# Order of work around fc2, the next image's layernorm and k's last tile in a fused transformer and ConvNeXt kernel

## The chip, the cores and the metric

The kernel runs on one core of a Trainium2 chip. The metric is the device time of one execution in microseconds (us). The kernel before ran beside each variant on the same chip; a comparison of two sets of runs goes by their ratios to it.

## The reference, cut to what matters

Eight images of 384 channels and 32 x 32 positions pass through an attention block with an MLP, then through a ConvNeXt block. All is float32.

```python
# layer 0, for each image: N = 1024 tokens, C = 384, 8 heads of 48, hidden 1536
xn  = layernorm(xf, g1, beta1)
q, k, v = split(einsum('bnc,oc->bno', xn, w_qkv) + b_qkv)
out = softmax(q @ k.T * 48 ** -0.5) @ v
x1  = einsum('bnc,oc->bno', out, w_proj) + b_proj + xf
h   = gelu(einsum('bnc,oc->bno', layernorm(x1, g2, beta2), w_fc1) + b_fc1)
y   = x1 + einsum('bnh,oh->bno', h, w_fc2) + b_fc2
# layer 1, on y as an image
z = layernorm(depthwise_conv_7x7(y) + dw_b, ln_w, ln_b)
z = gelu(z @ w1 + b1)
gx = sqrt(sum over positions of z ** 2);  nx = gx / (mean(gx) + 1e-6)
out = y + (grn_gamma * (z * nx) + grn_beta + z) @ w2 + b2
```

## The kernel before

TensorE does all matmuls; the 7 x 7 convolution of one image runs on VectorE (L769) beside the matmuls of the next. In fc2, w1 (called h) and w2, two thirds of the work is done by Strassen's scheme: products of blocks (A11, A12, S1 to S4, A22), for which VectorE must first subtract blocks of the activations (t1 to t4). The last third is done the plain way and is called "straight".

In these traces TensorE and VectorE work through their instructions in the order in which the program emits them: in the kernel before, a variance matmul that waits 3.74 us holds up the ready matmuls behind it. That order is set by a model clock: each group of matmuls calls `flow.pe(us)`, and "chains" (generators: the next image's layernorm, the block differences) emit their next instructions when the clock passes the pause that they yielded. A paced chain counts its pauses from its own last step, an unpaced one from the clock. The pauses therefore move instructions in the queues; they don't delay anything on the chip by themselves. Layernorm sums over channels, which lie on partitions, by a matmul with ones: `total` gives the mean and `var` the variance, so TensorE waits at these two if VectorE is late (28.5 and 33.5 us in the kernel before).

```python
# U = 0.857: model time in us of one full fp32 matmul of 512 columns
class Flow:
    def __init__(self):
        self.now, self.n, self.due, self.inside = 0.0, 0, [], False
    def pe(self, us):
        self.now += us
        if self.inside:
            return
        self.inside = True
        while self.due and self.due[0][0] <= self.now:
            at, _, chain, paced = heapq.heappop(self.due)
            self._step(chain, at, paced)
        self.inside = False
    def _step(self, chain, at, paced):
        wait = next(chain, None)
        if wait is not None:
            self.n += 1
            heapq.heappush(self.due, ((at if paced else self.now) + wait, self.n, chain, paced))
    def spawn(self, chain, paced=False):
        self._step(chain, self.now, paced)
        return chain
    def finish(self, chain):
        if chain is None:
            return
        self.due = [d for d in self.due if d[2] is not chain]
        heapq.heapify(self.due)
        inside, self.inside = self.inside, True
        for _ in chain:
            pass
        self.inside = inside
# ... (cut)
def layernorm(src, dst, h, eps, g, name, switch, spare=False, spaced=False):
    cols = half(h)
    if spare:
        a, *squares = (attn[:, i, :] for i in range(4))
        rstd = a
    else:
        a = one.tile([P, NH], F32, tag="ln_a", name=f"{name}_a{h}")
    nc.vector.tensor_tensor(a, src[:, 0, cols], src[:, 1, cols], ALU.add)
    nc.vector.tensor_tensor(a, a, src[:, 2, cols], ALU.add)
    yield 1.8
    total = o_tile(f"{name}_sum{h}")
    nc.tensor.matmul(out=total, lhsT=ones, rhs=a, start=True, stop=True)
    flow.pe(U)
    yield 0.8
    for ct in range(CT):
        nc.vector.scalar_tensor_tensor(dst[:, ct, cols], total, -1.0 / C, src[:, ct, cols], ALU.mult, ALU.add)
    yield 0.8
    if not spare:
        squares = [three.tile([P, NH], F32, tag="ln_sq", name=f"{name}_sq{h}_{ct}") for ct in range(CT)]
    for ct in range(CT):
        nc.scalar.activation(squares[ct], dst[:, ct, cols], AF.Square)
        if spaced:
            yield 1.7
    yield 0.8 if spaced else 1.8
    nc.vector.tensor_tensor(squares[0], squares[0], squares[1], ALU.add)
    nc.vector.tensor_tensor(squares[0], squares[0], squares[2], ALU.add)
    yield 1.8
    var = o_tile(f"{name}_var{h}")
    nc.tensor.matmul(out=var, lhsT=ones, rhs=squares[0], start=True, stop=True)
    flow.pe(U)
    yield 0.8
    if not spare:
        rstd = one.tile([P, NH], F32, tag="ln_rstd", name=f"{name}_rstd{h}")
    if switch:
        ln_table()
    nc.scalar.activation(rstd, var, AF.Ln, bias=eps, scale=1.0 / C)
    nc.scalar.activation(rstd, rstd, AF.Exp, scale=-0.5)
    yield 2.6 if switch else 1.2
    for ct in range(CT):
        nc.vector.scalar_tensor_tensor(dst[:, ct, cols], dst[:, ct, cols], col(g, ct), rstd, ALU.mult, ALU.mult)
def abreast(*args):
    chains = [layernorm(*args[:2], h, *args[2:], spare=(h == 1)) for h in range(2)]
    while chains:
        waits = []
        for chain in list(chains):
            wait = next(chain, None)
            if wait is None:
                chains.remove(chain)
            else:
                waits.append(wait)
        if waits:
            yield max(waits)
def both(*args):
    for h in range(2):
        yield from layernorm(*args[:2], h, *args[2:])
# ... (cut)
def qk(b, xn):
    big = one.tile([P, HT * N], F32, tag="big", name=f"qk_{b}")
    parts = big[:, : 2 * NP * N].rearrange("p (i m n) -> p i m n", i=2, m=NP)
    for m in range(CT):
        for i in range(2):
            at = i * CT + m
            def evict(dst, ps):
                nc.scalar.activation(dst, ps, AF.Identity, bias=bqk[:, at : at + 1], scale=1.0 if i else SCALE)
            args = lambda k: wqk_sb[:, k, at, :], lambda k: xn[:, k, :], CT
            if (m, i) != (CT - 1, 1):
                evict(parts[:, i, m, :], linear(*args, f"qk_{b}_{at}"))
                continue
            for h in range(2):
                evict(parts[:, i, m, half(h)], linear_half(*args, h, f"qk_{b}_{at}_{h}"))
    for i in range(2):
        for own, other in pieces(lambda m: parts[:, i, m, :]):
            nc.sync.dma_start(out=own, in_=other)
    return parts[:, 0], parts[:, 1]
# ... in attention(): ps_s has two buffers; scores() is one group of 4 matmuls and its exponential
steps = [(qh, m, t) for qh in range(2) for m in ORDER for t in range(KT)]
ln_table()
ln = None
for n in range(len(steps) + 2):
    if n < len(steps):
        ps[n] = scores(*steps[n])
    if n >= 2:
        product(*steps[n - 2], ps.pop(n - 2))
    # ... (cut)
# ... in the MLP: Strassen's form of fc2 for two thirds of the rows, "straight" for the last third
def down(hid, t1, weights, wname, first, add, done, name):
    h = HT // 2
    def block(s, n):
        return [hid[:, s * h + k, half(n)] for k in range(h)]
    def a(key):
        return [weights.at(wname, key)[:, k, :] for k in range(h)]
    def product(key, blocks):
        bank = o_tile(f"{name}_{key}")
        accumulate(bank, list(zip(a(key), blocks)))
        weights.used(wname, key)
        return bank
    straight = ps_s.tile([P, 2, NH], F32, tag="s", name=f"{name}_straight")
    for s, key in enumerate(("A31", "A32")):
        for k in range(h):
            for n in range(2):
                nc.tensor.matmul(
                    out=straight[:, n, :],
                    lhsT=a(key)[k],
                    rhs=block(s, n)[k],
                    start=s + k == 0,
                    stop=s == 1 and k == h - 1,
                )
            flow.pe(2 * U)
        weights.used(wname, key)
    for n in range(2):
        first(2, n, straight[:, n, :])
        done(2, n)
    b11, b12, b21, b22 = (block(s, n) for s in range(2) for n in range(2))
    t3, t2, t4 = b12, b11, b21
    def differences(dst, one_, other):
        for k in range(h):
            nc.vector.tensor_tensor(dst[k], one_[k], other[k], ALU.subtract)
            yield 1.2
    making_t3 = flow.spawn(differences(t3, b22, b12), paced=True)
    p1 = product("A11", b11)
    u2 = two.tile([P, NH], F32, tag="r", name=f"{name}_u2")
    nc.scalar.copy(u2, p1)
    for k in range(h):
        nc.vector.tensor_tensor(t2[k], b22[k], t1[k], ALU.subtract)
    first(0, 0, product("A12", b21))
    add(0, 0, u2)
    done(0, 0)
    making_t4 = flow.spawn(after(making_t3, differences(t4, b21, t2)), paced=True)
    p5 = product("S1", t1)
    first(1, 1, p5)
    first(0, 1, p5)
    add(0, 1, product("S4", b22))
    p6 = product("S2", t2)
    nc.vector.tensor_tensor(u2, p6, u2, ALU.add)
    add(0, 1, u2)
    done(0, 1)
    flow.finish(making_t3)
    p7 = product("S3", t3)
    u3 = two.tile([P, NH], F32, tag="r", name=f"{name}_u3")
    nc.vector.tensor_tensor(u3, p7, u2, ALU.add)
    add(1, 1, u3)
    done(1, 1)
    flow.finish(making_t4)
    first(1, 0, product("A22", t4))
    add(1, 0, u3)
    done(1, 0)
# ... in the loop over the images
def next_norms(b):
    if b > 0:
        acc = state["acc"]
        flow.finish(state["conv"])
        state["norm3"] = flow.spawn(
            sequence(abreast(acc, acc, eps1, "lnw", f"ln3_{b - 1}", True), block_differences(acc))
        )
    if b + 1 < B:
        xn = state["xn"] = load_x(b + 1, "xn")
        state["norm1"] = flow.spawn(
            after(state["norm3"], both(xn, xn, eps0, "g1", f"ln1_{b + 1}", True), 0 if b else 6)
        )
```

## Time and profile before

| | before |
|---|---|
| median of 3 runs, us | 3506.55 (3503.75 to 3507.19) |
| span of the profiled run, us | 3505.6 |
| TensorE busy | 97% |
| VectorE busy | 73% |
| ScalarE busy | 37% |
| ScalarE table loads | 79 |

How to read the lines in this document. A waits line says which engine and instruction (with its line in the kernel, such as L352) waited for which other: us in total, how many times, the longest. A timeline line has the start and the length in us, the engine, the line, the operation, what it wrote and read, its tile and how many records it covers; in brackets stands the idle time of that engine just before, and what ended it. One fp32 matmul is two records: the six of q/k's last tile are the 12 of L309 in the prediction's timeline. The kernel before and the changed one have different line numbers: L335 and L352 (mean and variance) before are L345 and L362 after; scores are L495 and L509; the reads of the straight product are L689 and L705. The lines of the kernel before are shown in the prediction.

### The profile page before, as it was taken

How to read it: one execution, taken by the hardware profiler on the slowest of the kernel's cores; microseconds unless marked ns; L12 is line 12 of the kernel's file. 1: busy time of each engine (PE TensorE's matmuls, PEld its weight loads, DVE VectorE, ACT ScalarE, POOL GpSimd, SP SyncE). 2: the span in 40 equal slices, each digit the busy share in tenths (PEclk: the TensorE clock that was granted, in tenths of full speed). 3: DMA queues.
4: the chain of work that ended last, by engine and by line, in shares of the span. 5: the costliest groups of instructions: out<-in, count | busy, mean ns of one | idle time of the engine just before them, and what ended most of it. 6: DMA issues, size and time to landing. Idle time of an engine off the chain costs nothing.

```text
span 3505.6 us, 36066 instructions
## 1 busy us (share of the span) xinstructions
PE 3397.9 (97%) x14106; PEld 1427.3 (41%) x14106; DVE 2548.4 (73%) x3176; ACT 1293.1 (37%) x1607; POOL 7.7 (0%) x21
## 2 busy tenths in 40 slices
PE   8999999999999999999999999999999999999978
PEld 3334434443344433444334443444434444344433
DVE  3243798677876878768686696857788679959974
ACT  3442353324533154341543405424253332532131
POOL 0000000000000000000000000000000000000000
PEclk9999999999999999999999999999999999999999
DMA  3312101221013200132002320022201312022111
GB/s 114 111 39 76 55 20 49 92 70 36 21 53 96 81 19 17 57 110 66 19 13 67 99 71 14 21 66 92 72 15 32 100 59 58 17 62 81 58 50 42
DMA packets 110688, 200.86 MB, mean 57 GB/s; under 512 B 30768, under 2 KB 37040, under 8 KB 110128
## 3 DMA queue, kind: packets, MB, share of 16 engines
q1 hardware_dynamic: 109936, 196.01, 19.1%
q8 instruction: 113, 1.85, 0.2%
q10 hardware_dynamic: 576, 2.48, 0.2%
q14 instruction: 63, 0.52, 0.1%
HBM read 160.16 MB, written 28.57 MB: 54 GB/s over the span
## 4 chain that ended last, share of the span: by engine, by line
PE 80%; DVE 14%; DMA 2%; ACT 2%; SPq 1%; issue 1%; DVEq 0%; ACTq 0%
PE fc L309 13%; PE h L316 11%; PE o L515 11%; PE s L495 10%; PE qk L296 6%; DVE wqkv L769 5%; PE o_straight L633 4%; PE o_S L316 4%; PE v L424 4%; PE fc_S L316 3%; PE o_A L316 3%; PE fc_straight L633 3%; PE proj L438 3%; DVE acc L769 2%; PE fc_A L316 1%; PE ln_var L352 1%
## 5 line engine op out<-in xcount | busy, mean ns | idle before, releaser
L769 DVE SCALAR_TENSOR_TENSOR acc<-pad,vec,acc 128x1024 f32<-128x1024 f32 x1008 | 1234.7, 1276 | 0.0
L504 ACT ACTIVATE p<-s 128x1024 f32<-128x1024 f32 x512 | 523.3, 1024 | 384.3 <-PE s L495 384.0
L495 PE MATMUL s<-qk 48*64 48x512 f32 x4096 | 532.8, 591 | 10.7 <-ACT p L504 10.7
L515 PE MATMUL o<-p,v 64*64 64x512 f32 x4096 | 530.6, 590 | 0.0
L309 PE MATMUL fc<-xn,fc 128*128 128x512 f32 x1152 | 500.9, 593 | 0.0
L817 DVE TENSOR_TENSOR y<-h,y 128x512 f32<-128x512 f32 x336 | 232.0, 691 | 138.3 <-PE h L316 123.7
L309 PEld LDWEIGHTS fc<-xn,fc 128*128 128x128 f32 x1152 | 218.1, 190 | 277.7 <-issue 274.8
L495 PEld LDWEIGHTS s<-qk 48*64 48x64 f32 x4096 | 153.1, 133 | 300.8 <-issue 271.4
L515 PEld LDWEIGHTS o<-p,v 64*64 64x64 f32 x4096 | 153.7, 132 | 288.0 <-issue 284.2
L600 ACT ACTIVATE hid<-fc,bfc_f 128x512 f32<-128x512 f32 x192 | 131.2, 687 | 361.1 <-PE fc L309 360.3
L296 PE MATMUL qk<-xn,wqkv 128*128 128x512 f32 x480 | 207.4, 592 | 0.0
L316 PE MATMUL h<-acc,w_A 128*128 128x512 f32 x432 | 204.0, 592 | 0.0
L402 ACT ACTIVATE qk<-qk,bqk 128x1024 f32<-128x1024 f32 (+1 forms) x56 | 55.6, 992 | 379.3 <-DVE acc L769 177.3
L769 DVE SCALAR_TENSOR_TENSOR wqkv<-pad,vec,wqkv 128x416 f32<-128x416 f32 (+1 forms) x288 | 191.6, 752 | 0.0
L456 DVE TENSOR_TENSOR attn<-o,attn 128x512 f32<-128x512 f32 x64 | 44.1, 689 | 196.6 <-ACT attn L454 196.6
L633 PE MATMUL o_straight<-y,w_A 128*128 128x512 f32 x336 | 148.5, 602 | 2.2 <-DVE w_A L895 2.2
L633 PE MATMUL fc_straight<-hid,fc_A 128*128 128x512 f32 x336 | 147.5, 592 | 0.0
L296 PEld LDWEIGHTS qk<-xn,wqkv 128*128 128x128 f32 x480 | 91.1, 190 | 114.1 <-issue 113.8
L795 ACT ACTIVATE y<-y,b_f 128x1024 f32<-128x1024 f32 x84 | 96.6, 1150 | 109.8 <-DVE y L817 109.8
L438 PE MATMUL proj<-attn,wproj_sb 128*128 128x512 f32 x288 | 131.4, 609 | 4.3 <-DVE attn L482 3.9
L424 PE MATMUL v<-wqkv,xn 128*128 128x384 f32 x384 | 128.9, 494 | 0.6 <-DVE xn L364 0.6
L316 PEld LDWEIGHTS h<-acc,w_A 128*128 128x128 f32 x432 | 82.1, 190 | 103.3 <-issue 84.7
(205 smaller groups left out, 3311.2 us busy)
## 6 DMA issues: line engine op xcount, KB each, us to landing
w_A<-in_w SPq DMA_DIRECT2D x96, 384.0 KB, 3.2
fc<-in_wfc SPq DMA_DIRECT2D x54, 384.0 KB, 3.4
fc_A<-in_wfc SPq DMA_DIRECT2D x47, 384.0 KB, 3.2
xn<-in_x SPq DMA_DIRECT2D x16, 768.0 KB, 6.7
x<-in_x SPq DMA_DIRECT2D x16, 768.0 KB, 6.6
kept<-x SPq DMA_DIRECT2D x8, 1536.0 KB, 5.8
res<-kept SPq DMA_DIRECT2D x48, 256.0 KB, 3.0
out_y<-res SPq DMA_DIRECT2D x48, 256.0 KB, 2.1
```

What stands on the lines that cost most here:

```text
L296: nc.tensor.matmul(out=ps[:, half(h)], lhsT=lhsT(k), rhs=rhs(k)[:, half(h)], start=(k == 0), stop=(k == nk - 1),)
L309: nc.tensor.matmul(out=ps, lhsT=lhsT(k), rhs=rhs(k)[:, half(h)], start=(k == 0), stop=(k == nk - 1))
L316: nc.tensor.matmul(out=bank, lhsT=lhsT, rhs=rhs, start=k == 0, stop=k == len(pairs) - 1)
L424: nc.tensor.matmul(out=ps[:, :C], lhsT=xn[:, k, t * P : (t + 1) * P], rhs=wv_sb[:, k, :], start=(k == 0), stop=(k == CT - 1),)
L438: nc.tensor.matmul(out=ps, lhsT=wproj_sb[:, m, ct * P : (ct + 1) * P], rhs=attn[:, m, :], start=(m == 0), stop=(m == CT - 1),)
L495: nc.tensor.matmul(out=s[64 * i : 64 * i + 64, j, :], lhsT=kT[64 * j : 64 * j + HD, m, k0 : k0 + 64], rhs=qT[64 * j : 64 * j + HD, m, half ...
L504: nc.scalar.activation(p, s, AF.Exp)
L515: nc.tensor.matmul(out=outs[i][64 * j : 64 * j + 64, :], lhsT=v[keys, t, at : at + 64], rhs=p[keys, j, :], start=(t == 0), stop=(t == KT - 1),
L600: nc.scalar.activation(hid[:, m, half(h)], ps, AF.Gelu, bias=bfc1[:, m : m + 1])
L633: nc.tensor.matmul(out=straight[:, n, :], lhsT=a(key)[k], rhs=block(s, n)[k], start=s + k == 0, stop=s == 1 and k == h - 1,)
L769: nc.vector.scalar_tensor_tensor(dst, window, tap, dst, ALU.mult, ALU.add)
L817: nc.vector.tensor_tensor(dst, bank, part, ALU.add)
```

## The change

The intent: (1) let the differences t2, t3 and t4 of fc2 leave VectorE one after the other in one paced chain, where t2 came as a bulk of six and t3 started beside it; (2) put the next image's layernorm at longer steps (most pauses times 1.8) and the convolution's layernorm too (all pauses times 1.4); the first pause is 2.6 for 1.8 in every layernorm, the second one of each image included; (3) compute k's last tile behind the first two score groups, so that the first exponentials run beside it; (4) leave out a table load of ScalarE where the table of Ln and Exp is still in place.

```diff
     def ln_table():
-        nc.scalar.preload_act_table_set("natural_log_exp_and_others")
-
-    def layernorm(src, dst, h, eps, g, name, switch, spare=False, spaced=False):
+        if table[0] != "ln":
+            nc.scalar.preload_act_table_set("natural_log_exp_and_others")
+        table[0] = "ln"
+
+    def other_table(dst, src, function, **kw):
+        nc.scalar.activation(dst, src, function, **kw)
+        table[0] = None
+
+    def layernorm(src, dst, h, eps, g, name, switch, spare=False, spaced=False, slow=1.0):
 ... (cut)
-        yield 1.8
+        yield 2.6 * slow
         total = o_tile(f"{name}_sum{h}")
 ... (cut)
-        yield 0.8
+        yield 0.8 * slow
 ... (cut)
-        yield 0.8 if spaced else 1.8
+        yield 0.8 if spaced else 1.8 * slow
         nc.vector.tensor_tensor(squares[0], squares[0], squares[1], ALU.add)
         nc.vector.tensor_tensor(squares[0], squares[0], squares[2], ALU.add)
-        yield 1.8
+        yield 1.8 * slow
 ... (cut)
-        yield 2.6 if switch else 1.2
+        yield (2.6 if switch else 1.2) * slow
 ... (cut: in abreast)
-                yield max(waits)
+                yield 1.4 * max(waits)
 ... (cut: in qk)
-                for h in range(2):
-                    evict(parts[:, i, m, half(h)], linear_half(*args, h, f"qk_{b}_{at}_{h}"))
-        for i in range(2):
-            for own, other in pieces(lambda m: parts[:, i, m, :]):
+        moves = [(own, other) for i in range(2) for own, other in pieces(lambda m: parts[:, i, m, :])]
+        for own, other in moves[:-2]:
+            nc.sync.dma_start(out=own, in_=other)
+
+        def last_tile():
+
+            for h in range(2):
+                evict(parts[:, 1, CT - 1, half(h)], linear_half(*args, h, f"qk_{b}_last_{h}"))
+            for own, other in moves[-2:]:
                 nc.sync.dma_start(out=own, in_=other)
 ... (cut: in attention)
         for n in range(len(steps) + 2):
+            if n == 2:
+                last_tile()
             if n < len(steps):
                 ps[n] = scores(*steps[n])
 ... (cut: GELU and square root now go through other_table)
 ... (cut: in down)
-        making_t3 = flow.spawn(differences(t3, b22, b12), paced=True)
         p1 = product("A11", b11)
         u2 = two.tile([P, NH], F32, tag="r", name=f"{name}_u2")
         nc.scalar.copy(u2, p1)
-        for k in range(h):
-            nc.vector.tensor_tensor(t2[k], b22[k], t1[k], ALU.subtract)
+        making_t2 = flow.spawn(differences(t2, b22, t1), paced=True)
+        making_t3 = flow.spawn(after(making_t2, differences(t3, b22, b12)), paced=True)
+        making_t4 = flow.spawn(after(making_t3, differences(t4, b21, t2)), paced=True)
         first(0, 0, product("A12", b21))
         add(0, 0, u2)
         done(0, 0)
-        making_t4 = flow.spawn(after(making_t3, differences(t4, b21, t2)), paced=True)
         p5 = product("S1", t1)
         first(1, 1, p5)
         first(0, 1, p5)
         add(0, 1, product("S4", b22))
+        flow.finish(making_t2)
         p6 = product("S2", t2)
 ... (cut: in next_norms)
-                    after(state["norm3"], both(xn, xn, eps0, "g1", f"ln1_{b + 1}", True), 0 if b else 6)
+                    after(state["norm3"], both(xn, xn, eps0, "g1", f"ln1_{b + 1}", True, slow=1.8), 0 if b else 6)
```

More of the change, by code (lines that the diff above doesn't have):

```diff
@@ L317, in accumulate @@
             flow.pe(U)
+    table = [None]
     def ln_table():
-        nc.scalar.preload_act_table_set("natural_log_exp_and_others")
-    def layernorm(src, dst, h, eps, g, name, switch, spare=False, spaced=False):
+        if table[0] != "ln":
[5 more added lines that the diff above has]
+    def layernorm(src, dst, h, eps, g, name, switch, spare=False, spaced=False, slow=1.0):
         cols = half(h)
@@ L377, in abreast, with both @@
             if waits:
-                yield max(waits)
-    def both(*args):
+                yield 1.4 * max(waits)
+    def both(*args, slow=1.0):
         for h in range(2):
-            yield from layernorm(*args[:2], h, *args[2:])
+            yield from layernorm(*args[:2], h, *args[2:], slow=slow)
     def pieces(at):
@@ L406, in qk @@
                     evict(parts[:, i, m, :], linear(*args, f"qk_{b}_{at}"))
-                    continue
-                for h in range(2):
-                    evict(parts[:, i, m, half(h)], linear_half(*args, h, f"qk_{b}_{at}_{h}"))
-        for i in range(2):
-            for own, other in pieces(lambda m: parts[:, i, m, :]):
+        moves = [(own, other) for i in range(2) for own, other in pieces(lambda m: parts[:, i, m, :])]
[5 more added lines that the diff above has]
+            for own, other in moves[-2:]:
                 nc.sync.dma_start(out=own, in_=other)
-        return parts[:, 0], parts[:, 1]
+        return parts[:, 0], parts[:, 1], last_tile
     def heads(t):
@@ L482, in average, with attention @@
         nc.vector.tensor_tensor(attn[:, m, :], attn[:, m, :], r, ALU.mult)
-    def attention(b, xt, qT, kT, xn, first=None):
+    def attention(b, xt, qT, kT, last_tile, xn, first=None):
         sums = two.tile([P, 2 * NP * 8], F32, tag="sums", name=f"sums_{b}")
@@ L599, in gelu_half @@
         ps = linear_half(lambda k: w[:, k, :], lambda k: xn[:, k, :], CT, h, f"{name}_{h}_{m}")
-        nc.scalar.activation(hid[:, m, half(h)], ps, AF.Gelu, bias=bfc1[:, m : m + 1])
+        other_table(hid[:, m, half(h)], ps, AF.Gelu, bias=bfc1[:, m : m + 1])
     def spare_blocks(name):
@@ L794, in finish @@
         def finish(m):
-            nc.scalar.activation(y[:, m, :], y[:, m, :], AF.Gelu, bias=b1[:, m : m + 1])
+            other_table(y[:, m, :], y[:, m, :], AF.Gelu, bias=b1[:, m : m + 1])
         def squares(i):
@@ L849, in grn_up_straight @@
                 ps = linear(lambda k: raw[:, tiles[k], :], lambda k: acc[:, k, :], CT, f"h_{b}_{m}")
-                nc.scalar.activation(y[:, m, :], ps, AF.Gelu, bias=b1[:, m : m + 1])
+                other_table(y[:, m, :], ps, AF.Gelu, bias=b1[:, m : m + 1])
                 nc.scalar.activation(ps, y[:, m, :], AF.Square, accum_out=gx[:, m : m + 1])
@@ L873, in grn_scale @@
         wb = f"w2_{tag}"
-        nc.scalar.activation(gx, gx, AF.Sqrt)
+        other_table(gx, gx, AF.Sqrt)
         yield 6.5
@@ L1145, in main @@
         for b in range(B):
-            qT, kT = qk(b, state["xn"])
+            qT, kT, last_tile = qk(b, state["xn"])
             if b == 0:
@@ L1150, in main @@
             xn = one.tile([P, CT, N], F32, tag="xn", name=f"xn2_{b}")
-            ln2, rest = attention(b, xt, qT, kT, xn, folding if b == 0 else None)
+            ln2, rest = attention(b, xt, qT, kT, last_tile, xn, folding if b == 0 else None)
             if b < B - 1:
@@ L1194, in exact_path @@
         with tc.For_i(0, B) as b:
+            table[0] = None
             weights = Weights(plan_fc1("x") + plan_fc2_fast("x") + plan_w1("x") + plan_w2("x"))
@@ L1198, in exact_path @@
             values("x", xn)
-            exact_attention(xt, *qk("x", xn))
+            qT, kT, last_tile = qk("x", xn)
+            last_tile()
+            exact_attention(xt, qT, kT)
             xn = one.tile([P, CT, N], F32, tag="xn", name="xn2_x")
```

## The prediction

> **What bounds the kernel now.** I read the page's busy shares and the slices of the span first, then the list of waits for TensorE alone, then the timeline around each wait.
>
> ```profile
> span 3505.6 us, 36066 instructions
> PE 3397.9 (97%) x14106; PEld 1427.3 (41%) x14106; DVE 2548.4 (73%) x3176; ACT 1293.1 (37%) x1607; POOL 7.7 (0%) x21
> ...
> PEclk9999999999999999999999999999999999999999
> ```
>
> TensorE is busy 97% of the span at a full granted clock. It is the bound, and all that a reordering can win lies in its 3505.6 - 3397.9 = 107.7 us of idle time. The reader should see from this alone that 2% (70 us) is out of reach unless two thirds of the idle time goes.
>
> The waits of TensorE (who, for whom: us in total, times, longest):
>
> ```profile
> PE ln_var L352 <- DVE ln_sq L349: 33.5, 11, 3.7
> PE ln_sum L335 <- DVE ln_a L332: 28.5, 11, 15.0
> PE s L495 <- ACT p L504: 10.7, 9, 1.2
> ```
>
> I placed every TensorE gap in the timeline. The start takes 15.3 us (load, first layernorm) and everything after the last image's fc2 42.5 us (the last convolution, the last scaling, the end); the change touches neither. The other 49.8 us are small gaps, of which these matter:
> - 1.24 us before the third score tile, once in each of 8 images: 9.9 us.
> - In fc2 of images 1 to 6, 3.74 us before the next layernorm's first variance sum (22.4 us) and, in four of them, 0.71, 0.85, 0.85 and 0.37 us before its second mean (2.8 us): 25.2 us. In image 0, 0.55 + 2.68 = 3.2 us.
> - In the second layernorm: 0.38, 0.62 and 1.50 us in image 1, 0.39 in image 6, 0.65 and 0.81 in image 7.
>
> The timeline of image 2's fc2 shows the 3.74:
>
> ```profile
> 1048.32 2.74 PE L316 MATMUL fc_A<-hid,fc_A 128*128 128x512 f32 x6
> ...
> 1050.89 1.40 DVE L689 SCALAR_TENSOR_TENSOR x<-fc_straight,vec,x 128x512 f32<-128x512 f32 x2
> 1051.03 1.13 PE L335 MATMUL ln_sum<-ln_a,ones 128*128 128x512 f32 x2
> ...
> 1057.01 3.69 DVE L659 TENSOR_TENSOR hid<-hid,fc_t 128x512 f32<-128x512 f32 x6
> ...
> 1062.01 0.69 DVE L349 TENSOR_TENSOR ln_sq<-ln_sq,ln_sq 128x512 f32<-128x512 f32 x1
> 1062.76 2.08 PE L352 MATMUL ln_var<-ln_sq,ones 128*128 128x512 f32 x2 [3.74 <-DVE ln_sq L349]
> ```
>
> VectorE has six block differences in a bulk (L659) and more of L651 ahead of the sum of squares, and TensorE meets the variance matmul before they are done.
>
> The timeline at the scores of image 3:
>
> ```profile
> 1249.48 1.11 ACT L402 ACTIVATE qk<-qk,bqk 128x1024 f32<-128x1024 f32 x1 [4.03 <-PE qk L296]
> ...
> 1254.63 0.69 ACT L402 ACTIVATE qk<-qk,bqk 128x512 f32<-128x512 f32 x1 [1.89 <-PE qk L309]
> 1255.34 1.28 ACT L320 ACT_TABLE_LOAD   x1
> 1256.63 1.94 ACT L504 ACTIVATE p<-s 128x1024 f32<-128x1024 f32 x2
> 1257.71 1.09 PE L495 MATMUL s<-qk 48*64 48x512 f32 x8 [1.24 <-ACT p L504]
> ```
>
> The third score tile needs the first one's buffer (there are two), and its exponential stands behind the last eviction and a table load.
>
> [...] L352 holds up the ready fc matmuls behind it for 3.74 us. So the order of instructions, which the changed program shows without running, decides the waits. [...] here the load takes 1.28 us and the exponential starts 1.29 us after it, so I count 1.28.
>
> **The change part by part.** Compared in order, both kernels have the same matmuls, the same VectorE instructions and the same transfers; only 23 table loads go (23 x 1.28 = 29 us of a ScalarE that is 37% busy, so worth something only where one stands in a chain). The rest is order.
>
> *k's last tile behind two scores.* Its six matmul pairs (two records of 0.43 us each, 6 x 0.86 = 5.15 us, as L309 shows) now stand between the second and the third score. The first exponential then has those 5.15 us to run in, and the 1.24 us go. But the second score now takes the buffer of the fifth q/k tile, just computed. Its eviction starts 0.20 us after the tile's end and takes 1.11, and restart costs 0.06: 1.37 us, against 0.86 us of the first score. A new wait of 0.51 us. Net 0.73 x 8 = **5.8 us**. The moved rows of that tile are first read by the ninth score, an estimated 9 us after its last eviction; the copies take some 3 us.
>
> *fc2, images 1 to 6.* The order shows more than the words of the change: the layernorm of the convolution is also paced by 1.4, so its last scaling (6 instructions), then the four block differences for w1, then the next image's first two adds (L331, L332) all come *behind* VectorE's two reads of the straight product (L689). Before, they came ahead of them (42.2 to 51.0 in the timeline). Those reads wait for the straight product's end. From that end, by rows of the timeline: 0.21 reaction, 1.32 for two L689, 4.1 for six scalings, 2.6 for four differences, 1.4 for the two adds, 0.06 to start: 9.7 us. TensorE has meanwhile A11 (6 pairs) and two of A12: 8 x 0.858 = 6.9 us before the mean's matmul. **A new wait of 2.8 us** takes the place of 3.74.
>
> I followed the same two queues further. First variance: VectorE does three t2 differences (1.9), the subtraction of the mean (2.0), two t2 (1.3), two for A12's result (1.4), one t2 and one t3 (1.2), two square adds (1.4): 18.9 us after the straight product's end, TensorE arrives at 20.0. No wait, 1.1 us to spare. Second mean: VectorE 30.1, TensorE 32.0. Second variance, now behind A22 and one h matmul: 39.3 against 42.3. Differences t2, t3 and t4 are ready 8, 6 and 4 us before S2, S3 and A22. Three layernorm instructions (2 us) move into h's first block, where VectorE needs some 9 of TensorE's 10 us and four banks give slack. So 25.2 - 6 x 2.8 = **8.4 us**.
>
> *fc2, image 0.* No convolution layernorm comes first; the mean stands 13.7 us behind the straight product's end where VectorE is done by 10.8, the variance later still: **3.2 us**.
>
> *Second layernorm.* The first pause grows from 1.8 to 2.6, which puts the mean one matmul later (0.86 us). That covers 0.38, 0.39 and 0.65 and 0.86 of 1.50; the variance moves along, so its waits stay: **2.3 us**.
>
> The end keeps its own 42.5 us: the last convolution runs back to back on VectorE behind the last fc2, and starts earlier by what was won. Sum: 5.8 + 8.4 + 3.2 + 2.3 = 19.7 us, so 3506.5 - 19.7 = 3487 us (-0.6%).
>
> **The rivals.**
> 1. *All of it goes.* If VectorE's chain is shorter than I count, or the wait is hidden, the gain is 9.9 + 25.2 + 3.2 + 2.3 = 40.6 us: 3466. For it: it is the intent. Against: eight matmul pairs can't cover 9.7 us of chain in an in-order queue, and each term is a measured row.
> 2. *The new wait before the mean is larger than the old, or the variance waits too.* With 1.1 us to spare there, a VectorE some 2 us later costs 1 us more in each of six images, and a mean's wait of 4 us another 7: about 3500. For it: VectorE is 73% busy and nearly full in this stage.
> 3. *ScalarE's order.* The exponentials and evictions near the last tile could push the third score, or the delayed root in h's first block delay a GELU. ScalarE at 37% speaks against; 1 us in each image would make 3495.
>
> **Range and chances.** The middle is 3487. The largest term is the 2.8 us, six times: at 0.8 it makes 3475, at 4.8 3499. Runs before lie within 3.4 us. So 3473 to 3499 for eight in ten. Faster by 2% needs 70 us of 107.7, of which the change touches about 43: 1 in 200. Slower by 2% would take a new wait of 10 us in each image: 1 in 100.
>
> **What would show it.** In the changed profile: no wait of a score for an exponential, and about 0.5 us of the second score for the eviction, 8 times; no 3.7 us before the variance; about 2.8 us before the first mean in images 1 to 6, with L689's successor ahead of the scalings; image 0 without waits; 56 table loads for 79; TensorE's busy time unchanged near 3398 and its idle time near 88 us. I am wrong if the first mean starts without a wait, if the variance still waits, or if busy time moves by more than a few us.

## The result and the profile after

| | before | after |
|---|---|---|
| median, us (4 runs each, same chip) | 3506.87 (3503.75 to 3507.9) | 3479.61 (3478.53 to 3480.27) |
| ratio | 1 | 0.9923 [0.9906, 0.9941] |
| TensorE busy, us | 3397.9 | 3388.2 |
| span minus TensorE busy, us | 107.7 | 90.2 |
| ScalarE table loads | 79 | 56 |

A ratio is the mean time of one kernel's runs over the mean of the other's of the same rounds, so it is not quite the ratio of the medians. The gain is 27.3 us by the medians, 0.8%.

The page of the changed kernel, its span, busy times and granted clock:

```profile
span 3478.4 us, 36056 instructions
...
PE 3388.2 (97%) x14106; PEld 1424.2 (41%) x14106; DVE 2545.8 (73%) x3176; ACT 1263.3 (36%) x1584; POOL 7.6 (0%) x21
...
PEclk9999999999999999999999999999999999999989
```

The number of matmul records is the same, 14106, and yet TensorE is busy 9.7 us less. The same matmuls got shorter. That is the first thing that the prediction did not have.

The waits of TensorE after:

```profile
PE ln_sum L345 <- DVE ln_a L342: 39.2, 10, 14.2
PE ln_var L362 <- DVE ln_sq L359: 10.4, 10, 3.5
PE b L222 <- DVE w_lnb L1058: 10.1, 1, 10.1
...
PE s L509 <- ACT qk L412: 1.5, 8, 0.2
```

The wait before the variance fell from 33.5 to 10.4 us, the one before the mean rose from 28.5 to 39.2, and a single wait of 10.1 us is new. The scores wait for an eviction now, eight times.

The timeline of the changed kernel in image 2's fc2, all engines, other lines left out:

```profile
1037.45 5.31 PE L649 MATMUL fc_straight<-hid,fc_A 128*128 128x512 f32 x12
...
1042.81 1.41 DVE L705 SCALAR_TENSOR_TENSOR x<-fc_straight,vec,x 128x512 f32<-128x512 f32 x2 [11.56 <-PE fc_straight L649]
1044.13 2.07 DVE L374 SCALAR_TENSOR_TENSOR acc<-acc,vec,ln_rstd 128x512 f32<-128x512 f32 x3
...
1051.47 0.69 DVE L342 TENSOR_TENSOR ln_a<-ln_a,xn 128x512 f32<-128x512 f32 x1
1052.31 1.10 PE L345 MATMUL ln_sum<-ln_a,ones 128*128 128x512 f32 x2 [2.68 <-DVE ln_a L342]
...
1060.34 0.69 DVE L359 TENSOR_TENSOR ln_sq<-ln_sq,ln_sq 128x512 f32<-128x512 f32 x1
...
1062.68 1.02 PE L362 MATMUL ln_var<-ln_sq,ones 128*128 128x512 f32 x2
```

VectorE stood idle for 11.56 us until the straight product was done, because its two reads of that product (L705) now come first in its queue. Then it had all of the scalings, the differences for w1 and the two adds to do, and TensorE waited 2.68 us for them. The variance (L362) no longer waits: its sum of squares was ready at 1061.03.

The timeline of the changed kernel at image 3's scores:

```profile
1239.85 1.09 PE L509 MATMUL s<-qk 48*64 48x512 f32 x8
...
1241.12 1.09 PE L509 MATMUL s<-qk 48*64 48x512 f32 x8 [0.19 <-ACT qk L412]
1242.14 5.42 PE L309 MATMUL qk_last<-xn,wqkv 128*128 128x512 f32 x12
...
1247.49 1.09 PE L509 MATMUL s<-qk 48*64 48x512 f32 x8
1248.40 1.04 PE L529 MATMUL o<-p,v 64*64 64x512 f32 x8
```

The third score no longer waits for an exponential. The second starts 1.27 us after the first, where 0.86 is the pace, so it lost 0.41.

I cut both traces into stages, from the first matmul of each stage to the first of the next. These are sums of mine over the traces, in us:

| stage | after minus before | the prediction |
|---|---|---|
| fc2 of images 1 to 6 (with h, since a variance matmul moved there) | -19.4 | -8.4 |
| fc2 of image 0 | -5.2 | -3.2 |
| q/k and attention, images 2 to 6 | -3.5, -0.69 each | -3.7, -0.73 each |
| image 0, q/k to fc1 | +2.2 | -0.7 |
| image 1, attention and fc1 | -1.6 + 1.9 | -2.0 |
| fc1 of images 2 to 6 | +1.2 | -0.4 |
| image 7, attention | -1.9 | -1.4 |
| start and end | -1.1 | 0 |
| sum | -27.4 (by the spans, -27.2) | -19.7 |

### The profile page after: what moved, and what is told of

The parts are those of the page before. It is cut to its first block, busy times and chain, and to the rows that moved or that the text cites. A ratio compares the mean times of both kernels' runs of the same rounds, so it can differ in the third digit from the quotient of the medians.

```text
span 3478.4 us, 36056 instructions
## 1 busy us (share of the span) xinstructions
PE 3388.2 (97%) x14106; PEld 1424.2 (41%) x14106; DVE 2545.8 (73%) x3176; ACT 1263.3 (36%) x1584; POOL 7.6 (0%) x21
## 4 chain that ended last, share of the span: by engine, by line
PE 84%; DVE 13%; DMA 1%; ACT 1%; SPq 1%; issue 1%; DVEq 0%; ACTq 0%
PE fc L309 12%; PE h L316 11%; PE s L509 11%; PE o L529 11%; PE qk L296 6%; DVE wqkv L785 5%; PE o_straight L649 4%; PE fc_straight L649 4%; PE o_S L316 4%; PE fc_S L316 4%; PE v L438 4%; PE o_A L316 3%; DVE acc L785 3%; PE proj L452 3%; PE fc_A L316 2%; PE ln_var L362 1%
## 5 line engine op out<-in xcount | busy, mean ns | idle before, releaser
L316 PE MATMUL h<-acc,w_A 128*128 128x512 f32 x432 | 204.9, 592 | 0.0
L412 ACT ACTIVATE qk<-qk,bqk 128x1024 f32<-128x1024 f32 x40 | 44.5, 1114 | 352.6 <-DVE acc L785 177.3
L316 PEld LDWEIGHTS h<-acc,w_A 128*128 128x128 f32 x432 | 82.1, 190 | 103.3 <-issue 83.5
```

The source lines that it names most:

```text
L316: nc.tensor.matmul(out=bank, lhsT=lhsT, rhs=rhs, start=k == 0, stop=k == len(pairs) - 1)
```

## The experiments

Twelve kernels ran, all correct, all in five rounds against the kernel before. They came in three sets of four; the medians of the kernel before were 3505.91, 3506.51 and 3507.74 us. The first two sets (e1 to e4, e5 to e8) ran on one chip and share nine runs of the kernel before; the third ran on another. The theory to test: a wait of TensorE costs more than its recorded idle time, since its clock drops to half afterwards (the shortening of the same matmuls; in image 2 of before the trace grants 0.50 from 1062.19 to 1065.60 us), and the change's own pace of the convolution's layernorm makes the 2.68 us. The rival: idle time is all there is, and the excess lies in the parts that I mis-sized.

The reason to suspect the clock is this table of two stretches of the kernel before in image 2's fc2, the wait of 3.74 us and the 3.2 us after it, and a third, later one. Columns: stretch, its us, busy time (instructions) of TensorE, weight loads, VectorE, ScalarE and GpSimd, then TensorE's granted clock, DMA share, GB/s.

```profile
1059.02:1062.76 3.74, 0.00 (x1) 0.00 (x1) 3.58 (x6) 0.00 (x0) 0.00 (x0) 0.92 0.00 0
1062.76:1065.97 3.21, 3.21 (x4) 1.43 (x5) 0.00 (x0) 1.07 (x2) 0.00 (x0) 0.56 0.00 0
1065.97:1070.00 4.03, 4.03 (x11) 1.87 (x10) 3.72 (x6) 0.89 (x2) 0.00 (x0) 1.00 0.22 65
```

The same view of the changed kernel, the wait of 2.68 us and the 3.2 us after it:

```profile
1049.63:1052.31 2.68, 0.00 (x1) 0.03 (x1) 2.65 (x6) 0.00 (x0) 0.00 (x0) 1.00 0.29 114
1052.31:1055.52 3.21, 3.21 (x8) 1.54 (x9) 3.21 (x6) 0.92 (x2) 0.00 (x0) 1.00 0.00 0
```

In the same 3.21 us, four matmul records pass before and eight after. TensorE was "100% busy" both times. Before, the granted clock was 0.56 there. In the trace's clock records the half-clock stretches in fc2 last 3.41 us, in image 4 of before 6.83; before, they follow the wait in images 0, 1, 2, 4, 5 and 6 but not in image 3; after, only in image 1.

### e1_last_tile: k's last tile alone

The kernel before with only this part of the change:

```diff
 ... (cut: the edits in qk, as in the change)
+            if n == 2:
+                last_tile()
```

> The kernel before with only k's last tile moved behind the first two scores. My theory: from one marker to the next, the q/k and attention stages of images 2 to 6 became 0.69 us shorter each in the changed kernel, so eight images give -5.5 us; but the preparation in image 0 is now spawned 5.1 us of TensorE work earlier against the scores, and its column sums meet a load that has not landed (10.1 us wait in the changed kernel), which costs some 5.6 us. Sum: 0 us, between -2 and +2. Rival (my prediction's term alone, with the 10.1 us wait coming from the other parts): -5.8 us.

Measured: 3504.5 us, ratio 0.9997 [0.9984, 1.0011]. Attention of the later images got 0.69 us shorter each, as in the change. Image 0 gave it back, with 7.1 us more from q/k to fc1: the wait before L222 came up there too, at 10.8 us, so this part alone brings it. The prediction's 5.8 us for this part are about right image by image and worth nothing in sum.

### e2_chain: the paced chain alone

```diff
-        making_t3 = flow.spawn(differences(t3, b22, b12), paced=True)
-        for k in range(h):
-            nc.vector.tensor_tensor(t2[k], b22[k], t1[k], ALU.subtract)
+        making_t2 = flow.spawn(differences(t2, b22, t1), paced=True)
+        making_t3 = flow.spawn(after(making_t2, differences(t3, b22, b12)), paced=True)
+        making_t4 = flow.spawn(after(making_t3, differences(t4, b21, t2)), paced=True)
 ... (cut: the old making_t4 goes, t2 is finished before S2)
```

> The kernel before with only the fc2/w2 differences in one paced chain t2, t3, t4. My theory: the next image's layernorm then stands ahead of most differences on VectorE, the 3.74 us waits before the variance and the stretches of half clock behind them go, and no 2.7 us wait before the mean appears, as the convolution's layernorm keeps its place ahead of the straight product: -30 us, between -24 and -38, more than the whole change won (27 us). Rival: the chain and the longer steps are needed together, and the chain alone leaves a wait of about 2 us or more before the variance: -15 us or less.

Measured: 3471.45 us, ratio 0.9903 [0.9887, 0.9918], so 34 us less by the ratio. Its waits:

```profile
PE ln_sum L335 <- DVE ln_a L332: 26.8, 13, 14.4
...
PE ln_var L352 <- DVE ln_sq L349: 8.5, 5, 3.5
```

The six waits of 3.74 us before the variance are gone, and nothing of their size took their place. fc2 takes 64.56 us in each of images 1 to 6 (before 68.85 to 70.64), at a full clock. By its median this one part wins more than the whole change.

### e3_steps: the longer pauses alone

```diff
-        yield 1.8
+        yield 2.6 * slow
 ... (the other pauses times slow, slow=1.8 for the next image)
-                yield max(waits)
+                yield 1.4 * max(waits)
```

> The kernel before with only the longer pauses in all layernorms (1.8 times for the next image, 1.4 times for the convolution's, 2.6 for 1.8 in the first). My theory: the bulk differences stay ahead of the layernorm on VectorE, so a wait of about 3.4 us before the mean is added and one of about 2.6 us before the variance stays: no gain, between -3 and +12 us. Rival: the longer steps are what removed the 3.74 us waits: -15 us or more.

Measured: 3496.85 us, ratio 0.9978 [0.9964, 0.9991]: about 8 us less, outside what I expected. Its waits:

```profile
PE ln_sum L336 <- DVE ln_a L333: 42.9, 9, 14.3
PE ln_var L353 <- DVE ln_sq L350: 18.1, 14, 3.5
```

In each of images 1 to 6 there is now a wait of 3.28 us before the mean, and in images 2 to 5 one of 1.84 before the variance. In these four the two are 5.12 us, more than the 3.74 plus at most 0.85 of before, and over all six the listed idle time is 27.0 us for 25.2; still these stages are 3.9 us shorter in sum. The clock dropped in images 1 and 6 only. If idle time were all, as the rival says, they would have become longer.

### e4_warm: the same wait, with TensorE kept at work in it

The kernel before, with four useless matmuls ahead of the first variance matmul in images 1 to 6. Their result is overwritten by the right one.

```diff
         var = o_tile(f"{name}_var{h}")
+        if h == 0 and name in ("ln1_2", "ln1_3", "ln1_4", "ln1_5", "ln1_6", "ln1_7"):
+            for _ in range(4):
+                nc.tensor.matmul(out=var, lhsT=ones, rhs=dst[:, 0, cols], start=True, stop=True)
```

> The kernel before with four extra matmuls (3.4 us of useless work, same order otherwise) in front of the next image's first variance matmul in images 1 to 6, where TensorE waits 3.74 us; results stay right, as the real matmul overwrites them. Theory of the clock: the wait itself costs only part, TensorE's clock is halved for 3.4 or 6.8 us after it (five of six waits in the trace before)[...]; with work in the wait the clock stays, so -7 us, between -5 and -11, and no halved clock in those stages. Rival (only the idle time costs[...]): 0 us, between -1 and +1.

Measured: 3498.28 us, ratio 0.9984 [0.9971, 0.9998]. The interval reaches nearly to the rival's "no change", so the trace decides. Image 2's fc2:

```profile
1055.00 3.60 PE L354 MATMUL ln_var<-xn,ones 128*128 128x512 f32 x8
1058.90 1.12 PE L355 MATMUL ln_var<-ln_sq,ones 128*128 128x512 f32 x2 [0.31 <-DVE ln_sq L349]
1059.86 1.02 PE L316 MATMUL fc_A<-hid,fc_A 128*128 128x512 f32 x2
```

The two fc matmul records behind the variance (L316) take 1.02 us as a pair at the full clock (1.51 in the kernel before, at 1064.63 us), and no half-clock stretch is left in fc2 of images 1 to 6 (image 0, which has no extra matmuls, keeps its own). fc2 is 68.83 us in all six images, the same as the one image of before without a drop (68.85). The six together are 412.98 us for 419.67: 6.7 us come from the clock, though nothing else in these stages was made faster and TensorE had 24 matmuls more to do. This is a net figure: a TensorE that isn't slowed comes earlier to the second mean and waits 0.84 us there in all six images, 5.0 us for the 2.8 of before.

### e5_no_stretch: the change without the factor of 1.4

```diff
-                yield 1.4 * max(waits)
+                yield max(waits)
```

> The changed kernel with the convolution's layernorm at its old pace (1.0 for 1.4), all else kept. My theory: its last scaling, the four differences for w1 and the next image's two adds return ahead of VectorE's reads of the straight product, so the 2.68 us wait before the mean goes in images 1 to 6 and no wait takes its place: 6 x (2.68 + some 0.3 of stopping and restarting) = 18 us less than the changed kernel, 45 us less than before, between -40 and -50. Rival: the wait only moves to the variance or the second mean (VectorE is the bound of this stage): within 5 us of the changed kernel, so -22 to -32 against before.

Measured: 3462.35 us, ratio 0.9878 [0.9863, 0.9894]. Timeline of image 2's fc2:

```profile
1036.82 5.31 PE L316 MATMUL fc_A<-hid,fc_A 128*128 128x512 f32 x12
1038.10 0.69 DVE L342 TENSOR_TENSOR ln_a<-ln_a,xn 128x512 f32<-128x512 f32 x1
1038.71 1.40 DVE L705 SCALAR_TENSOR_TENSOR x<-fc_straight,vec,x 128x512 f32<-128x512 f32 x2
...
1041.97 1.02 PE L345 MATMUL ln_sum<-ln_a,ones 128*128 128x512 f32 x2
```

With the shorter pace the adds (L342) lie ahead of the reads of the straight product (L705) again, VectorE does them while TensorE works, and the mean waits for nothing. fc2 takes 63.52 us in all six images and h the 56.65 of the kernel before, so I use this stage below as the one without waits. This one factor costs the change 16 to 17 us.

### e6_first_pause: the first pause back to 1.8

```diff
-        yield 2.6 * slow
+        yield (2.6 if slow > 1 else 1.8) * slow
```

> The changed kernel with the first pause of the second layernorm back at 1.8 (2.6 and its factors kept for the next image's). My prediction's term: the longer pause wins 2.3 us, so this kernel loses 2.3. Reading of the two traces: the longer pause costs 1.0 us in all (it moves a wait onto the variance in fc1), so this kernel is 1 us faster than the changed one, -28 against before, too small to settle by time; the stages of the trace decide.

Measured: 3461.83 us, ratio 0.9874 [0.9859, 0.9889]: a miss. I meant the second layernorm alone, but the condition also covers the convolution's layernorm, whose first pause shrank with it. The 2.68 us were gone as in e5 (fc2 and h together 120.17 us in both). So its time shows the convolution's pace again, by another handle, and says nothing of the second layernorm. Its stages do say something: fc1 takes 71.46 us in image 2, for 71.79 in the changed kernel.

### e7_late_prep: image 0's preparation spawned later

In image 0 the weights are prepared beside attention: small column sums (L222) wait for a product on VectorE. In the changed kernel the load for it is issued at 148.13 us, 2.4 after TensorE stopped, and VectorE stands idle for 10.06 us until 153.72, when the attention's own sums, ahead of the product in its queue, have come by DMA. The changed kernel's wait of 10.1 us lies there. First the kernel before at that place:

```profile
158.09 2.08 PE L438 MATMUL proj<-attn,wproj_sb 128*128 128x512 f32 x2 [3.35 <-DVE attn L482]
159.96 1.28 PE L222 MATMUL b<-ones,w_lnb 128*128 128x1 f32 x6
```

The changed kernel:

```profile
144.72 1.04 PE L509 MATMUL s<-qk 48*64 48x512 f32 x8
155.84 1.44 PE L222 MATMUL b<-ones,w_lnb 128*128 128x1 f32 x6 [10.09 <-DVE w_lnb L1058]
```

k's last tile is now part of attention's model time, so the model clock reaches the column sums some groups of scores earlier, ahead of the projection instead of inside it. The edit delays them by the length of that tile:

```diff
-                folding = flow.spawn(folds(weights))
+                folding = flow.spawn(after(None, folds(weights), 2 * CT * U))
```

> The changed kernel with the preparation of the folded biases spawned 5.1 us of TensorE work later in image 0, where it stood against the scores before the change. My theory of the 10.1 us wait in image 0: spawned before the last q/k tile's 5.1 us are counted, its column sums were emitted three score steps earlier than the load they need allows. With the old distance the wait returns to some 3 to 4 us before the projection: -6 us against the changed kernel, between -4 and -8. Rival: the wait comes from the transfers themselves being later (another order in the queue), and does not move: 0.

Measured: 3481.82 us, ratio 0.9936 [0.992, 0.9951], no gain over the change by time; its six runs spread over 17 us. The 10.1 us are gone; 4.11 us before a projection matmul and 1.14 in fc1 came instead. Image 0's attention and fc1 took 227.1 us, for 225.6 in the changed kernel. The idea that this wait is worth its own length falls: it replaced waits of 3.35, 1.48 and 0.51 us (5.3 in all) that the kernel before has at the projections and column sums. The edit did take 4.0 us of listed idle time from image 0 (q/k to fc1), but in this profile half clock took 11.5 us from the matmuls there, for 7.0 in the changed kernel.

### e8_all: e5, e6 and e7 together

```diff
-                yield 1.4 * max(waits)
+                yield max(waits)
-        yield 2.6 * slow
+        yield (2.6 if slow > 1 else 1.8) * slow
-                folding = flow.spawn(folds(weights))
+                folding = flow.spawn(after(None, folds(weights), 2 * CT * U))
```

> The three edits together: convolution's layernorm at the old pace, first pause 1.8, preparation at the old distance. If they are independent: -18 - 1 - 6 = -25 us against the changed kernel, 52 us less than before (about 3454 us where before takes 3506), between -46 and -57.

Measured: 3456.57 us, ratio 0.986 [0.9845, 0.9875]. It beats both kernels and is the fastest by median, 49 us under before by the ratio.

### e9_pause_ln2: the first pause of the second layernorm alone

```diff
-        yield 2.6 * slow
+        yield (1.8 if name.startswith("ln2_") else 2.6) * slow
```

> The changed kernel with the shorter first pause (1.8) in the second layernorm alone; the edit meant for this before also shortened the convolution's. My prediction's term: +2.3 us. Reading of the traces: the longer pause costs 1.0 us over the eight images, so -1 us against the changed kernel (-28 against before), with the fc1 stage of images 2 to 6 at 71.45 us for 71.79 and the 2.68 us waits in fc2 still there. If those waits go here as well, it was not the convolution's pace that removed them.

Measured: 3480.86 us, ratio 0.9927 [0.9913, 0.994], the change's own time. fc1 takes 71.46 us again in images 2 and 5, as before, and 71.70 and 71.56 in 3 and 4, for the change's 71.79, and the 2.68 us are still there. So the longer pause in the second layernorm costs up to a third of a microsecond an image in fc1, where the prediction counted a gain, and e6's gain came from the convolution's pace.

### e10_tables: the table loads back

```diff
-        if table[0] != "ln":
-            nc.scalar.preload_act_table_set("natural_log_exp_and_others")
+        nc.scalar.preload_act_table_set("natural_log_exp_and_others")
```

> The changed kernel with every table load put back (79 for 56, 23 x 1.28 us of ScalarE). Theory: ScalarE waits for others in all these places, so TensorE's waits stay as they are and the time is that of the changed kernel within 2 us (-27 against before). Rival: the loads stood in the chain from a variance to the scaled activations, and their return lengthens the wait before the mean by 1 us or more in images 1 to 6: +6 us or more against the changed kernel.

Measured: 3480.45 us, ratio 0.9932 [0.9918, 0.9945]. ScalarE is busy 1294.2 us for 1263.3 and TensorE's waits are nearly the same (38.7 us before the mean and 10.6 before the variance, for 39.2 and 10.4). Leaving out 23 table loads is worth nothing on the path.

### e11_pace_pause: e5 with e9's edit

```diff
-                yield 1.4 * max(waits)
+                yield max(waits)
-        yield 2.6 * slow
+        yield (1.8 if name.startswith("ln2_") else 2.6) * slow
```

> The changed kernel with the convolution's layernorm at its old pace and the second layernorm's first pause at 1.8, the preparation as the change has it. If moving the preparation won nothing (as the stages of its two runs say), this equals the kernel with all three edits: -49 us against before, between -44 and -53. If it is 5 us slower than that one, the preparation's place did win something.

Measured: 3460.67 us, ratio 0.987 [0.9855, 0.9885]. It differs from e8 by 4.1 us of median, in another set on another chip, with intervals that overlap, so I leave open whether e8 is truly better. The traces speak for it: image 0 from q/k to fc1 takes 254.7 us here and 251.4 in e8, with 12.1 and 7.3 us of listed idle time, while fc2 and h are alike. So the preparation's later place may be worth some 3 us.

### e12_chain_tile: chain and last tile, without the longer pauses

The kernel before with the edits of e1 and e2:

```diff
+            if n == 2:
+                last_tile()
-        making_t3 = flow.spawn(differences(t3, b22, b12), paced=True)
+        making_t2 = flow.spawn(differences(t2, b22, t1), paced=True)
+        making_t3 = flow.spawn(after(making_t2, differences(t3, b22, b12)), paced=True)
 ... (cut: the rest as in e1 and e2)
```

> The kernel before with only the paced chain of differences and k's last tile moved: no longer pauses anywhere, no table kept. The chain alone gave -34 us. The tile adds 8 x -0.69 us and some 3 to 8 us of image 0's new wait: -35 us against before, between -31 and -40. The longer steps of the next image's layernorm are then worth the rest of what the best kernel wins, some 10 us, of which 6 x 1.04 us stand in the fc2 stage (64.56 us with the chain alone, 63.52 with longer steps too).

Measured: 3470.86 us, ratio 0.9899 [0.9884, 0.9914]; fc2 takes 64.57 us. This stands apart from the change with its loads back in the same set (e10, 0.9918 at the least), by medians 9.6 us. The chain and the tile add up (e1 and e2 give the same); the pauses then cost 9 us on top of them, though they won 8 alone. Inside the pauses, the factor of 1.4 costs 16 to 17 us, as e5 shows, and the rest, with the table loads, wins some 7 (e12 against e5 by their ratios, as they come from different sets).

## Why the prediction was right or wrong

The time, 3479.6 us, lies in the range of 3473 to 3499, but the middle was 7 us too high, and behind that lie larger errors of opposite sign. That the sum came so near is in part luck.

**The waits of fc2: right in place, wrong in price.** The prediction named the new wait before the mean (2.8 us; measured 2.68, six times), put L705 ahead of the scalings, and gave the variance 1.1 us to spare (measured 1.6). It then wrote "25.2 - 6 x 2.8 = 8.4 us", and the stage gave 19.4. The step that failed is that a wait was priced at its recorded idle time. With e5's stage, which has no wait, as the zero, the excess of the six stages is:

| us, images 1 to 6 | before | after |
|---|---|---|
| stage above that of e5 | 38.6 | 19.2 |
| of it listed idle time | 25.2 | 16.1 |
| of it half clock, in the matmuls | 9.4 | 1.7 (image 1) |
| the rest | 4.0 | 1.4 |

So the gain of 19.4 is 9.1 idle, 7.7 clock and 2.6 of a rest. The clock part is shown: e4 takes it away with the wait filled, and image 3 of before, the one without a drop, says the same without any edit. (e4's stages win only 6.7 us, because 2.3 us of other waits come back there.) The rest lies at the stops too. A matmul record at the full clock is 0.592 us long while matmuls start every 0.429 (fc2 of image 2 from 1066.40 us), so by starts a stop is some 0.16 us longer than its recorded idle time: 4.33 us from the last start to the variance's, less 0.43, are 3.90 for 3.74. By starts, image 3 of before has three stops and no other delay: in each the second record of the matmul with ones also starts 0.08 to 0.10 us late, and the stop before the first mean is 0.13 us, too short to be listed. Together this rest is 0.74 us there; behind the one wait of after it is 0.24. Image 0's fc2 is the same mis-sizing: 3.2 predicted, 5.2 measured, with one half-clock stretch less (1.4 us of it in the matmuls).

**What the trace before showed and I did not use.** The row of the variance matmul that the prediction quotes has 2.08 us for its two records, where another pair of L352 takes 1.02 (at 1039.73 us). That should have raised the question of the clock at once. The prediction read a "full granted clock" from the slices of the span, and they can't show it: a slice is 88 us, and 3.4 us at half clock in it take 2% off its mean. At half clock matmuls started every 0.853 us for 0.429 (image 2, 1063.77 to 1065.48), so I estimate 1.7 us lost in a recorded stretch of 3.413, half of it; what the matmuls of fc2 lost before agrees: 1.4 to 1.7 us in images with one stretch (which can lie partly in the wait itself), 2.9 in image 4 with 6.83 us, none in image 3. The term "TensorE's busy time unchanged near 3398" failed for the same reason: 9.7 us less, since matmuls at half clock are recorded longer (1.06 us for 0.592 there). In fc2 and h of images 0 to 6 it is 12.2 us less, 9.2 of them by the clock; the end of the program has 2 us more.

**Scores: right, by two errors that cancel.** Predicted 1.24 - 0.51 = 0.73 us an image, measured 0.69. The second score lost 0.41, not 0.51. The last tile among the scores also costs 0.16 us going in and 0.20 coming out (1.02 for 0.86, and 5.35 for 5.15); full 128-row tiles stand between 48 x 64 tiles there, and no run isolates the cause of the two. And the removed wait was 1.46 by starts (3.18 us from the first score to the third, less 1.72), for 1.24 recorded.

**Image 0: "image 0 without waits" did not hold.** The prediction followed the waits of fc2 there, but not the column sums of the preparation, which the order of the two programs would have shown moved. The net cost is some 3 us beside the scores' 0.7. It is only 3 of 10 us because other waits went: the listed idle time from q/k to fc1 rose from 7.3 to 11.0 us. The rest is the clock again. In all fourteen profiles this stretch takes 234 us (within 0.6), plus its listed idle time, plus what half clock took from its matmuls: 8.1 us before, 7.0 in the changed kernel, 7.0 to 11.5 in the variants. So e7 won 4.0 us of waiting and lost 4.5 to the clock. Kernels with the same order of matmuls up to there differ too (a stretch of 3.4 us in the changed kernel and of 10.2 in e9, both near 100 us), so one profile of image 0 is good to some 3 us only.

**The second layernorm had the wrong sign.** Predicted -2.3, measured about +1: image 7 won about 1, image 1 lost about 1, fc1 of images 2 to 6 lost 1.2 with a new wait of the variance of 0.18 us and more in image 6. The step "that covers 0.38, 0.39 and 0.65" held for the mean, but the variance moved from a place without a wait to one with. e9 gives the 0.33 us an image back.

**Rivals.** The first (all waits go, 40.6 us) was argued against rightly for this change, since its order makes VectorE late. But e5 shows that one factor stood in the way: without it all of fc2's waits go and the time is 43 us lower. The second and third did not come true: the new wait is 2.68 us, the variance has time to spare, and the table loads were rightly counted as worth nothing (e10).

## What to carry to other kernels

Price a wait of the bound engine by the stage's length with and without it, not by its listed idle time: here a stage with 25.2 us of idle time had 38.6 us to win, because the clock fell to half behind five of its six waits of 3.74 us (9.4 us) and each stop is longer than its listed time (4.0 us). Where an engine takes its instructions in order, put no read that must wait ahead of work that is ready: one pace of 1.4 moved VectorE's reads of a late product in front and cost 16 us. Test the parts of a bundled change alone and in pairs; the longer pauses won 8 us by themselves and cost 9 beside the paced chain.

## What the traces show of stops and the clock

- Behind a wait of 3.74 us in fc2 the clock halved for 3.41 us in images 1, 2, 5 and 6 of before, for 6.83 in image 4, and not at all in image 3. Shorter waits had it too: one of 2.68 us in image 1 of the changed kernel (fc2 67.27 us for 65.58 in the other five), one of 2.68 in image 0 of before, and 3.28 in two of six images in e3. So the length of a wait alone doesn't tell whether the clock drops, and 2.68 us can be enough.
- What a stop in a stream of matmuls cost while the clock stayed full: 0.24 to 0.27 us above the listed idle time at each listed stop of fc2. The stops make 4.0 of 38.6 us of excess before.
- Records of 0.592 us at a pace of 0.429 make each idle time in fc2 0.16 us too short, and a half clock shows as more busy time (9.4 us in fc2 of images 1 to 6 before), not as idle time.
- Around one full tile among 48 x 64 tiles TensorE lost 0.16 and 0.20 us (image 3 of the changed kernel).
- A table load of ScalarE takes 1.28 us. In image 3 of before the next activation started 1.29 us after the load began, and 23 loads more cost ScalarE 30.9 us, 1.34 each (e10).
